# Where the score units of the next image stand: two of them moved ahead of the second group norm

## The chip, the cores and the metric

The kernel runs on one core of a Trainium2 chip. A core has five engines that run beside each other, each with its own instruction stream: TensorE for matmuls (PE in the profile, its weight loads PEld), VectorE (DVE), ScalarE (ACT), GpSimd (POOL) and SyncE (SP), which issues most of the DMAs. The engines wait for each other by semaphores. The metric is the device time of one execution in microseconds (us).

## The reference, cut to what matters

Input and output are four images of 256 channels by 64 x 64 pixels, f32. Two layers follow each other.

```python
# layer 0: attention over all 4096 pixels of an image
q = einsum('oc,bcn->bno', wq, xf) + bq            # 32 channels
k = einsum('oc,bcn->bon', wk, xf) + bk
attn = softmax(einsum('bnd,bdm->bnm', q, k), axis=-1)
v = einsum('oc,bcn->bon', wv, xf) + bv
x = gamma[0] * einsum('bcn,bmn->bcm', v, attn) + x
# layer 1
y = x + ls1 * cluster(group_norm(x, gn1_w, gn1_b), ...)
hdn = conv1x1(group_norm(y, gn2_w, gn2_b), mlp_w1, mlp_b1)      # 256 -> 1024
y = y + ls2 * conv1x1(gelu(hdn), mlp_w2, mlp_b2)                # 1024 -> 256
z = relu(batch_norm(y * dw_w, ...))
z = relu(batch_norm(conv1x1(z, pw_w), ...))                     # 256 -> 256
```

A group norm takes mean and variance over all channels and pixels of one image, so nothing behind it can start before the last pixel is there.

## The kernel before, in words

An image of 4096 pixels is cut into eight blocks of 512 (`NBLK`, `NB`). The four images go through three stages each: the attention's weighting, the cluster part, and the multilayer part (`mlp`, L1514), which holds the two 1 x 1 convolutions with the GELU between them, and the pointwise convolution. Every instruction of an engine stands in the order in which the Python code records it: nothing is moved by a scheduler. The order is written out by hand, and work of the next image is put between work of this one.

**Score units.** The attention's scores of an image are computed in 64 units: eight query blocks by eight key groups (`GRP`). A unit has two halves of 128 x 1024 scores, each two matmuls of 128 x 512 (`products`, L415) into one of two banks of the pool `ps_s` (each 128 x 2 x 512), and ACT copies each half into a buffer in SBUF (`kept`, L432). `score(u, hooks, later)` (L470) first calls `begun(u)` (L400), which issues the load of the *next* unit's key tile on SP (`k_unit`, L394, L398; two buffers for key tiles), then issues the matmuls of both halves, the first copy, and leaves the second copy in `hooks` and the running maximum over keys in `later`: four DVE instructions a unit (L492), two for unit 0. The first eight units of an image belong to its first query block; for images 1 to 3 they are computed during the previous image's stages, unit 0 at the end of its cluster part (L1393) and units 1 to 7 in its multilayer part.

**The end of the cluster part.** `cluster` adds its result to the image tiles in sixteen pieces. For half of them ACT scales the matmul's result (L1362) and POOL adds it (L1363), for the other half DVE does both (L1350). DVE then takes statistics of each piece (L1331). Between them, `fill(n)` runs parts of the next image's value projection (L375). Unit 0 of the next image comes last, and `cluster` returns.

**The second group norm (gn2).** `group_norm` (L270) combines the statistics on DVE (L274), averages over partitions by two tiny matmuls (L276, L277), and after one more average (L287), a square root on ACT (L199) and a reciprocal it gives scale and shift. `fill` puts value projections between. Then `norm(0)` scales block 0 (L1547) and forms differences of its quarters (L1614 to L1617).

**The multilayer part.** For each block `nb` there are four steps `j`, one for a quarter of the hidden channels, written (nb, j) below. `first` (L1683) does the first convolution of a step by `seven` (L1715), seven products of 128 x 256 in place of eight, in three banks of `ps_s`; DVE adds the parts (L1725) and ACT applies the GELU (L1689). `second_by_seven` (L1643) does the second convolution of the step before in seven products (L1651) and some sums on POOL (L1658 to L1663); `slots` says how many of those seven stand at which of four places inside the next `first`: (0, 2, 2, 3) or, behind a score, (3, 1, 2, 1). After step 0, `finish` adds the block before into the image tile (L1780), and after step 1 its ReLU runs on ACT (L1771) and the input of the block after is formed by DVE (`norm(nb + 1)`, L1547) and POOL. Step 2 is followed by the pointwise convolution of the block before, and the output leaves by DMA (L1607).

The dictionary `at` (L1825) says behind which step which score unit is computed:

```python
at = {(u, 3): u for u in range(1, 7)} | {(7, 2): 7}
if blocks < NBLK:                       # image 2: its last block is done later
    at |= {(6, 1): 6, (6, 2): 7}
    del at[6, 3]
```

The maxima that `score` leaves in `maxima` are taken out one at a time by `rest()` (L1818), four a block in blocks 0 to 6, around steps 2 and 3.

**Buffers.** The score buffers, the image tiles (two blocks each), the inputs of the blocks (`xn2`) and some others share one pool, `spool`, of 13 buffers of 8 KB a partition. A tile gets a buffer when it is first asked for, in the order of the code, and the first instruction that writes it waits until the last reader or writer of the buffer's former tile is done.

## Time and profile before

| what | value |
|---|---|
| median of 3 runs | 3199.19 us (3198.45 to 3201.14) |
| profiled execution: own time, span | 3196.98 us, 3195.0 us |
| PE busy | 3085.5 us, 97% of the span |
| DVE busy | 2537.0 us, 79% |
| POOL busy | 2260.6 us, 71% |
| ACT busy | 1734.8 us, 54% |
| granted TensorE clock, mean | 0.99 |

The profile is of one execution, and all its times count from the start of the span. A line of it names the engine, the line of the kernel, the tile written and those read; in brackets behind a line of the timeline stands how long the engine had been idle, and what ended that. The multilayer parts of images 0, 1 and 2 begin with the first product of block 0 at 623.6, 1408.9 and 2197 us. [...] a product of 128 x 256 (two passes) starts 0.43 us after the one before when nothing holds it up.

### The profile page before, as it was taken

What the parts mean: (1) busy time and instruction counts of PE and PEld (TensorE: products, weight loads), DVE (VectorE), ACT (ScalarE), POOL (GpSimd) and SP (SyncE); (2) the same over time, 40 slices, a digit from 0 to 9 for tenths busy, and PEclk for the clock granted to TensorE, in tenths of its full rate; (3) what the DMA queues carried; (4) which work ended last, traced back from release to release, by engine and by line L of the source; (5) the groups of instructions that cost most, each with busy time, mean ns of one, the idle gap of its engine ahead of it and who ended that gap; (6) DMA issues with size and microseconds to landing.
All of it is one profiled execution on the core that took longest, in us unless ns stands there. A gap on an engine that the chain in (4) does not pass through costs nothing.

```text
span 3195.0 us, 40473 instructions
## 1 busy us (share of the span) xinstructions
PE 3085.5 (97%) x13890; PEld 2445.7 (77%) x13890; DVE 2537.0 (79%) x3649; ACT 1734.8 (54%) x2719; POOL 2260.6 (71%) x2127
## 2 busy tenths in 40 slices
PE   7999999999999999999999999999999999998999
PEld 5777887788677787768867788786876787875786
DVE  3888888677788888867778888877778888887675
ACT  4556654545556665445555666544556566654444
POOL 3888886378488888547848888855766888883663
PEclk8999999999999999999999999999999999999999
DMA  5122126100112123510011222431111112150000
GB/s 164 40 63 63 60 61 182 63 21 30 47 50 63 53 60 94 155 50 28 23 56 44 66 60 63 111 123 50 30 44 43 54 60 64 56 149 2 14 21 27
DMA packets 105868, 200.33 MB, mean 63 GB/s; under 512 B 14416, under 2 KB 30400, under 8 KB 104128
## 3 DMA queue, kind: packets, MB, share of 16 engines
q1 hardware_dynamic: 101856, 181.94, 17.9%
q0 software_dynamic: 2976, 14.70, 2.5%
q8 instruction: 110, 1.80, 0.2%
q10 hardware_dynamic: 832, 1.11, 0.1%
q14 instruction: 94, 0.77, 0.1%
HBM read 149.37 MB, written 48.34 MB: 62 GB/s over the span
## 4 chain that ended last, share of the span: by engine, by line
PE 42%; POOL 24%; DVE 19%; issue 8%; ACT 6%; DMA 1%; POOLq 0%; SPq 0%; ACTq 0%; DVEq 0%
PE mo L1651 10%; POOL acc L595 9%; PE av L679 6%; PE hq L1734 5%; DVE top L444 5%; DVE s L583 4%; POOL t L595 4%; POOL s L595 4%; DVE t L616 3%; PE hp L1734 3%; PE hr L1734 3%; PE fv L1225 3%; PE sc L420 3%; POOL acc L611 2%; PE vp L375 2%
## 5 line engine op out<-in xcount | busy, mean ns | idle before, releaser
L433 ACT COPY s<-sc 128x1024 f32<-128x1024 f32 x512 | 514.8, 1011 | 506.3 <-PE sc L420 500.1
L583 DVE TENSOR_TENSOR s<-s,hold 128x1024 f32<-128x1024 f32 x512 | 598.7, 1209 | 28.9 <-ACT hold L566 15.0
L595 POOL TENSOR_TENSOR s<-t,s 128x512 f32<-128x512 f32 x224 | 303.5, 1355 | 356.1 <-DVE t L616 287.6
L679 PE MATMUL av<-t,v 128*128 128x256 f32 x1792 | 464.8, 382 | 12.8 <-DVE t L616 11.7
L679 PE MATMUL av<-s,v 128*128 128x256 f32 x1792 | 460.8, 379 | 2.2 <-ACT s L589 2.2
L595 POOL TENSOR_TENSOR acc<-acc,t 128x512 f32<-128x512 f32 x352 | 461.2, 1329 | 0.0
L679 PE MATMUL av<-s,sum 128*128 128x256 f32 x1792 | 459.5, 379 | 0.0
L420 PE MATMUL sc<-q,k 128*128 128x512 f32 x1024 | 405.6, 480 | 36.8 <-DMA k<-k 10.5
L444 DVE TENSOR_TENSOR top<-sc,top 128x1024 f32<-128x1024 f32 x326 | 397.8, 1220 | 29.7 <-ACT s L433 24.8
L1689 ACT ACTIVATE hs<-hs,pv_s 128x256 f32<-128x256 f32 x496 | 232.3, 502 | 343.5 <-DVE hs L1725 343.5
L616 DVE TENSOR_TENSOR t<-s,hold 128x1024 f32<-128x1024 f32 x224 | 272.7, 1217 | 159.3 <-ACT s L592 71.0
L679 PEld LDWEIGHTS av<-t,v 128*128 128x128 f32 x1792 | 338.4, 190 | 70.1 <-DVE t L616 21.4
L1651 PE MATMUL mo<-hs,w 128*128 128x256 f32 x1512 | 385.3, 381 | 0.0
L679 PEld LDWEIGHTS av<-s,v 128*128 128x128 f32 x1792 | 340.3, 190 | 57.8 <-ACT s L589 2.6
L679 PEld LDWEIGHTS av<-s,sum 128*128 128x128 f32 x1792 | 339.4, 189 | 54.5 <-issue 1.9
L1651 PEld LDWEIGHTS mo<-hs,w 128*128 128x128 f32 x1512 | 283.0, 190 | 47.2 <-ACT hs L1689 6.4
L595 POOL TENSOR_TENSOR t<-s 128x512 f32<-128x512 f32 x224 | 295.7, 1320 | 17.6
L420 PEld LDWEIGHTS sc<-q,k 128*128 128x128 f32 x1024 | 176.6, 190 | 144.0 <-DVE top L444 70.2
L592 ACT ACTIVATE s<-s 128x1024 f32<-128x1024 f32 x256 | 267.5, 1045 | 1.2
L1725 DVE TENSOR_TENSOR hs<-hq,hs 128x256 f32<-128x256 f32 x496 | 198.8, 421 | 79.2 <-PE hq L1734 69.3
L588 ACT ACTIVATE hold<-s 128x512 f32<-128x512 f32 x224 | 135.1, 603 | 221.5 <-DVE s L583 221.4
L679 PE MATMUL av<-t,sum 128*128 128x256 f32 x896 | 231.7, 381 | 0.0
(299 smaller groups left out, 5349.1 us busy)
## 6 DMA issues: line engine op xcount, KB each, us to landing
k<-k SPq DMA_DIRECT2D x256, 256.0 KB, 2.7
x<-in_x SPq DMA_DIRECT2D x62, 512.0 KB, 6.6
out<-xn SPq DMA_DIRECT2D x62, 256.0 KB, 2.1
att<-t SPq DMA_DIRECT2D x56, 256.0 KB, 3.9
x<-att POOLq DMA_DIRECT2D x12, 1024.0 KB, 8.7
q<-q SPq DMA_DIRECT2D x32, 256.0 KB, 4.1
w<-in_w SPq DMA_DIRECT2D x8, 1024.0 KB, 10.3
rden<-row_rd SPq DMA_DIRECT2D x28, 256.0 KB, 3.7
```

Of the source, the lines that this page charges most:

```text
L420: nc.tensor.matmul(sc[:, r, :], k_s[:, (2 * h + r) * P : (2 * h + r + 1) * P], qs[u // GRP], start=True, stop=True,)
L433: nc.scalar.copy(slots[u][:, PAIR[h]].rearrange("p h r n -> p r h n"), tiles(sc))
L444: nc.vector.tensor_tensor(top, src, top if saved[nb] is None else saved[nb], ALU.max)
L583: nc.vector.tensor_tensor(sh, sh, mb.to_broadcast([P, 2, 2, QW]), ALU.subtract)
L592: nc.scalar.activation(s[:, PAIR[1]], s[:, PAIR[1]], AF.Exp)
L595: nc.gpsimd.tensor_tensor(out, x, y, op)
L616: nc.vector.tensor_tensor(t31[u], s[:, B11 : B22 + 1 : 2], b12.to_broadcast([P, 2, 2, QW]), ALU.add)
L679: nc.tensor.matmul(av[bank][:, half_ * QW : (half_ + 1) * QW], a[:, r], t[:, r], start=(g == 0 and r == 0 and i in (1, 7, 2, 4)), stop=(g ...
L1651: return nc.tensor.matmul(bank[:, half * HB : (half + 1) * HB], a[:, j], t, start=start, stop=stop)
L1689: nc.scalar.activation(src, src, AF.Gelu_apprx_tanh, bias=pvc("b1", P, j + 4 * (i > 1)))
L1725: nc.vector.tensor_tensor(dst, ps, term, ALU.add)
L1734: nc.tensor.matmul(out, w, x, start=True, stop=True)
```

## The change

Units 1 and 2 of the next image are computed right behind unit 0, at the end of `cluster`, and thus ahead of gn2's matmuls on TensorE and ahead of gn2's work on ACT; their key loads, and that of unit 3, come earlier on SP. In the multilayer part, five steps and not seven have a score behind them (four and not six of the steps (u, 3), and (7, 2) as before; for image 2, three and not five, and (6, 1) and (6, 2) as before): units 3 and 4 move up to the steps (2, 3) and (3, 3), and the steps (1, 3) and (4, 3) have none. The `slots` of the steps behind these two change with that. The maxima of units 1 and 2 wait in `maxima` with those of unit 0, so `rest()` finds work from block 0 on, and none in block 5.

```diff
+EARLY = 3
...
         nxt.q_block(0)
         nxt.k_unit(0)
         fill(1)
-        copies = []
-        nxt.score(0, copies, maxima)
-        copies.pop()()
+
+        for u in range(EARLY):
+            copies = []
+            nxt.score(u, copies, maxima)
+            copies.pop()()
         return stats2
...
-        at = {(u, 3): u for u in range(1, 7)} | {(7, 2): 7}
+        at = {(2, 3): 3, (3, 3): 4, (5, 3): 5, (6, 3): 6, (7, 2): 7}
         if blocks < NBLK:
             at |= {(6, 1): 6, (6, 2): 7}
             del at[6, 3]
```

Line numbers of the changed kernel are three higher up to L1392 and five higher behind it.

## The prediction

> **What bounds the kernel now.** I read the page's first two parts, then who waited for whom with TensorE as the waiter, then the timeline around the second group norm (gn2) of image 0, and then busy time by stretch.

> ```profile
> PE 3085.5 (97%) x13890; PEld 2445.7 (77%) x13890; DVE 2537.0 (79%) x3649; ACT 1734.8 (54%) x2719; POOL 2260.6 (71%) x2127
> ...
> PE gnm_gn L276 <- DVE mv_gn L274: 12.8, 3, 4.3
> ```

> TensorE is busy 97% of the span, so a change pays only if it takes matmul time out of a saturated stretch or fills one of the few holes. The second line is such a hole: three times, once for each image that has a successor, TensorE stands 4.26 us before the first matmul of gn2.

> ```profile
> 609.55 7.21 DVE L1331 BATCH_NORM_STATS2 st<-x 128x6 f32<-128x512 f32 x12
> ...
> 610.30 0.81 PE L420 MATMUL sc<-q,k 128*128 128x512 f32 x2
> ...
> 612.29 1.94 ACT L433 COPY s<-sc 128x1024 f32<-128x1024 f32 x2
> ...
> 612.44 0.73 PE L420 MATMUL sc<-q,k 128*128 128x512 f32 x2 [1.33 <-ACT cl L1362]
> ...
> 616.79 0.59 DVE L274 BATCH_NORM_AGGREGATE mv_gn<-st 128x2 f32<-128x96 f32 x1
> ...
> 617.43 0.59 PE L276 MATMUL gnm_gn<-mv_gn,left 128*128 128x1 f32 x2 [4.26 <-DVE mv_gn L274]
> ```

> The hole lasts from 613.17 to 617.43, and DVE's statistics end it. Unit 0's four score matmuls stand ahead of it; ACT copies each half out in 0.97.

> ```profile
> 613.20:617.40 4.20, 0.00 (x0) 0.00 (x0) 4.14 (x7) 1.03 (x2) 4.12 (x4) 0.88 0.00 0
> 617.40:623.60 6.20, 6.17 (x18) 5.24 (x19) 2.90 (x11) 2.18 (x4) 2.96 (x3) 0.53 0.00 0
> 623.60:636.20 12.60, 12.60 (x74) 8.61 (x73) 7.96 (x20) 5.78 (x12) 3.32 (x5) 1.00 0.46 166
> ```

> Columns: length, busy time (count) of PE, PEld, DVE, ACT, POOL, then the granted clock. After the idle stretch the clock is 0.53: the hole costs more than its length. The same pair stands at 1403 (0.56) and 2191 (0.52).

> [...] the clock halves at 616.39, after a 3.41 us window with under 0.05 us of matmul, and returns at 623.21. [...] the 256 KB key loads (L398) land 2.4 at least, 2.7 median, 4.5 at most after issue. [...]

> **The change, part by part (for one image; three have it).**

> *Removed from the multilayer part:* the scores behind steps (1,3) and (4,3). From the starts of the first product of each step: a scored step 3 takes 7.05 and the next step 0 4.77, together 11.8. Image 3 has no scores and takes the slot pattern that these two steps now get: 4.75 + 6.04 = 10.79. So 1.0 each, **-2.0**. After block 0, the step 0 of an unscored pattern took 6.51, 0.47 over, because a POOL factor (L1615) came late. At (4,3) POOL's factor ends at 761.77 and would be needed at about 762.3; bounds 0 to 0.47, I take **+0.1**.

> *Added ahead of gn2:* eight matmuls, four ACT copies, two key loads. Copies of unit 0 end at 613.26 and 614.23, so unit 1's halves run at 613.3 and 614.3 (two matmuls of 0.215 each), their copies end at 615.2 and 616.2. Unit 2 needs key tile 2, whose buffer unit 0 frees at 613.17; nothing stands before it on SP until 629.6, so it lands near 615.9. Its four matmuls issue by 616.8, 0.6 ahead of 617.43; the last copy ends near 618.7, ahead of ACT's next work (620.40). gn2's statistics are DVE's and POOL's and don't move. Cost **0**, hidden by the hole; each us by which the key lands later than 2.7 + 0.6 delays gn2 by one us (4.5: +1.2); below nothing it can't be.

> *Moved on DVE:* eight maxima of 0.69 to blocks 0 and 1. Step 2 with maxima takes 10.71, without 10.54. Block 1 now pays that 0.17, block 5 no longer does; block 0's step 3 has DVE gaps of 1.27. Sum **0** (bounds -0.2 to +0.3).

> *A buffer wait that the diff doesn't show:* two more of the 13 big buffers are taken before gn2, and the built program gives the input of block 5 the buffer of the image tile with blocks 2 and 3, last read by the relu of block 3 on ACT. In the trace DVE writes block 5's first half at

> ```profile
> 747.08 1.41 DVE L1547 TENSOR_SCALAR xn<-x,ga_gn,gb_gn 128x512 f32<-128x512 f32 x2
> 748.40 1.21 DVE L492 TENSOR_TENSOR top<-top,s 128x512 f32<-128x512 f32 x1
> ...
> 747.79 0.80 ACT L1771 ACTIVATE xn<-x,dw_e,dw_d 128x512 f32<-128x512 f32 x1
> ```

> and the relu ends at 748.59: DVE now stands 1.56. Behind it queue the second half, a maximum and step 2's additions; the first of these (749.53 to 749.95) frees the bank of TensorE's matmul at 750.63. With the maximum at its usual 0.75 the addition ends near 751.1, TensorE loses 0.47; with 1.2 it loses 0.75. The pointwise part has a stall of 0.12 to absorb. **+0.5**, bounds 0 and 1.56. The new waits of unit 4 and of blocks 3 and 4 on an output's DMA have a step or more in hand, as block 5's own unit has now: 0.

> *The clock:* with the hole filled the clock may stay full. An estimate from the trace: counting 0.215 a pass, the window at 2111 (about 0.36 busy) dropped the clock and the one at 2183 (0.38) didn't. A half unit is 0.43, so a 3.41 us window passes with three halves (0.378) and fails with two. Halves would lie at 610.3, 612.4, 613.3, 614.3, 615.9 and 616.4; sliding the window over them, somewhat under half of the positions catch only two. If the clock holds: gn2's first matmuls reach DVE in 0.7 (as gn1's do) rather than 1.06, the four passes of value projection before gnv (L287) take 0.9 rather than 1.9, so the statistics are ready 1.4 earlier, and the second product of block 0, at 624.05 now, waits only for DVE's L1615, ending at 623.77 - 1.37: **-1.5** (bounds -1.6 and 0).

> Sum for one image: -2.0 + 0.1 + 0 + 0 + 0.5 = **-1.4** with the clock dropped, **-2.9** with it held. Three images: -4.2 to -8.7; held in two of three, **-7.2**. On the profiled execution, whose span is 3195.0 and own time 3196.98, this gives 3187.8 and 3189.8; the median shown is 3199.19, 2.2 above that execution, so 3192.0.

> **Rivals.**

> *Clock drops anyway.* For: gaps of 1.7 (before unit 0's second half) and 1.2 (before key tile 2) remain, and the margin is one half unit. Against: the 0.38 window. -4.2 to -5.7 with one held: 3195.0 to 3193.5, within 0.2%.

> *The buffer wait eats it.* For: DVE has no gap from 741 to 749 in that block. If all 1.56 reaches TensorE: -2.0 + 0.1 + 1.56 = -0.3, about -1 in three: 3198 (3194 with the clock held). Against: TensorE has 0.7 of slack before the bank it needs.

> *The key load becomes the gate (slower).* [...] gn2 stands behind unit 2's matmuls, and those behind key tile 2. Landing L after 613.17, gn2 is late by L - 3.3, and the clock drops too. The 1.4 is gone at L = 4.7; slower by 0.2% (6.4 us) takes L = 6.9: 3206. Against: the longest of 256 key loads was 4.5, and no DMA runs between 600 and 629.

> **How the numbers follow.** About 0.2% (6.4 us) is what a measurement of this kernel tells from no change. Clock held in two or three images: 0.5 (3190.5 to 3192.0). Clock dropped in most: 0.3. Buffer wait in full: 0.1. Key load: 0.04. The rest, 0.06, is mostly a gain that I haven't seen. So faster 0.55, same 0.40, slower 0.05. Range: low with all clocks held and buffer and POOL waits nothing, -3.5 x 3 = -10.5, 3188.7, rounded to 3189.0; high 3198.5, just past the buffer rival.

> **What would show it.** The row "gnm_gn <- mv_gn" falls from 12.8 to under 2; eight L420 matmuls lie between 613 and 617; the clock in the 6 us after gn2's first matmul is 1.00 where it held; the steps behind (1,3) and (4,3) add to 10.8; a new wait of DVE L1547 on ACT L1771 of about 1.5, three times. I am wrong if gn2's first matmul starts later against the last statistics than now, if block 4's step 2 loses over 1 us, or if gn2 keeps the clock low in all three while the total still falls by 7.

## The result, and the profile after

The changed kernel takes 3192.68 us (median of 12 runs, 3188.03 to 3198.69), the kernel before beside it 3199.59 (12 runs, 3197.33 to 3203.37). The ratio is 0.9977, with a 95% interval of 0.997 to 0.9985: faster by 0.23%. The profiled execution of it has a span of 3188.8 us and an own time of 3191.02; that of before had 3195.0 and 3196.98.

The first part of the page has the same instructions on every engine as before; TensorE is busy 5.3 us less, in a span that is 6.2 shorter:

```profile
PE 3080.2 (97%) x13890; PEld 2442.4 (77%) x13890; DVE 2539.7 (80%) x3649; ACT 1734.9 (54%) x2719; POOL 2257.7 (71%) x2127
```

TensorE's waits (total, times, longest) show that the hole ahead of gn2 is gone. The row had 12.8 us in three waits:

```profile
PE gnm_gn L279 <- DVE mv_gn L277: 0.6, 2, 0.4
```

The timeline of the changed kernel at the same place in image 0 (start, length, engine, line, ..., in brackets the idle time before it):

```profile
612.73 0.82 PE L423 MATMUL sc<-q,k 128*128 128x512 f32 x2
...
614.71 3.77 ACT L436 COPY s<-sc 128x1024 f32<-128x1024 f32 x4
614.87 0.73 PE L423 MATMUL sc<-q,k 128*128 128x512 f32 x2 [1.32 <-ACT cl L1365]
615.63 2.15 SPq L401 DMA_DIRECT2D k<-k  x2
615.78 0.73 PE L423 MATMUL sc<-q,k 128*128 128x512 f32 x2 [0.18 <-ACT s L436]
616.70 0.73 PE L423 MATMUL sc<-q,k 128*128 128x512 f32 x2 [0.19 <-ACT s L436]
...
618.42 1.17 PE L423 MATMUL sc<-q,k 128*128 128x512 f32 x4 [0.99 <-DMA k<-k]
...
619.86 0.38 PE L279 MATMUL gnm_gn<-mv_gn,left 128*128 128x1 f32 x2 [0.27 <-DVE mv_gn L277]
```

The two units lie in the hole as forecast: unit 1's halves follow ScalarE's copies, unit 2 waits for its key tile, which is there 2.8 us after its load was issued, and gn2 starts 7.13 us after unit 0, exactly as before. What follows is the busy time by stretch, for image 0 and for image 2. The columns are PE, PEld, DVE, ACT, POOL, then the granted clock:

```profile
612.70:619.80 7.10, 4.21 (x14) 1.94 (x12) 7.07 (x12) 6.20 (x9) 6.90 (x6) 1.00 0.29 74
619.80:625.50 5.70, 4.47 (x21) 3.46 (x22) 3.70 (x14) 3.93 (x7) 3.04 (x3) 1.00 0.00 0
...
2177.50:2185.00 7.50, 5.36 (x14) 2.88 (x13) 7.09 (x12) 6.25 (x9) 7.28 (x6) 0.76 0.25 72
2185.00:2191.40 6.40, 6.40 (x19) 5.32 (x18) 3.23 (x12) 3.53 (x6) 2.69 (x3) 0.50 0.00 0
```

In images 0 and 1 the clock stayed at 1.00, in image 2 it fell to 0.50, as it had fallen in all three before. There the matmuls of unit 2 itself ran at the low clock (its four took 2.05 against 1.17 in image 0), and gn2 came 0.35 later. In the traces of before and after every stretch of one granted clock that ends inside the span lasts a whole multiple of 3.413 us (1 to 579 of them); such a piece of 3.41 us is called a window here.

To say where the time went, I put the starts of the same matmuls of both executions side by side and took the differences of successive ones. All three images agree to 0.02 outside gn2's own stage:

| stretch | before | after | difference, image 0 / 1 / 2 |
|---|---|---|---|
| unit 0 to the first product of (0, 1): hole and gn2 | 20.00 | 18.82 | -1.18 / -1.08 / +0.54 |
| step (1, 0) | 6.51 | 6.85 | +0.34 / +0.33 / +0.32 |
| step (1, 2) | 10.54 | 10.72 | +0.18 each |
| steps (1, 3) and (2, 0) | 11.78 | 10.79 | -0.99 / -1.01 / -1.01 |
| step (4, 2) | 10.71 | 11.03 | +0.32 / +0.31 / +0.31 |
| steps (4, 3) and (5, 0) | 11.82 | 10.95 | -0.87 / -0.85 / -0.86 |
| step (5, 2) | 10.72 | 10.53 | -0.19 each |
| unit 0 to the next image's first weighting product | 250.74 | 248.28 | -2.46 / -2.36 / -0.78 |

The columns before and after are image 0's. The last row adds to -5.6 in three images; the other 0.6 of the span is a balance of differences elsewhere, where the programs are the same (+2.4 ahead of image 0's unit 0, -1.2 and -2.4 in the weighting and cluster parts of images 1 and 2, +0.5 in the last image). Part of it lies where the clock fell in one execution and not in the other; I didn't follow the rest.

Two losses were in it. The first I had seen coming; it is the wait of VectorE at the input of block 5, in the timeline of image 0:

```profile
748.52 0.80 ACT L1776 ACTIVATE xn<-x,dw_e,dw_d 128x512 f32<-128x512 f32 x1
...
749.35 1.41 DVE L1552 TENSOR_SCALAR xn<-x,ga_gn,gb_gn 128x512 f32<-128x512 f32 x2 [1.46 <-ACT xn L1776]
...
751.75 1.13 PE L1739 MATMUL hr<-xn,w 128*128 128x256 f32 x4 [0.23 <-DVE hs L1730]
```

The relu ends at 749.32, VectorE has then stood 1.46, and of that TensorE loses about 0.3. The second I had missed. It is at the head of block 1:

```profile
649.00 0.73 POOL L1619 TENSOR_TENSOR xn<-xn 128x256 f32<-128x256 f32 x1
649.37 0.92 DVE L495 TENSOR_TENSOR top<-top,s 128x512 f32<-128x512 f32 x1
...
649.82 1.05 POOL L1620 TENSOR_TENSOR xn<-xn 128x256 f32<-128x256 f32 x1
...
650.92 0.70 PE L1739 MATMUL hp<-xn,w_abcd 128*128 128x256 f32 x2 [0.54 <-POOL xn L1620]
```

A maximum that now stands behind first(0, 3) runs on VectorE at the moment when GpSimd forms the second factor of block 1. That factor takes 1.05 where it took 0.72 before, and the second product of the block waits for it 0.54 instead of 0.20, as in this line of before:

```profile
649.33 0.70 PE L1734 MATMUL hp<-xn,w_abcd 128*128 128x256 f32 x2 [0.20 <-POOL xn L1615]
```

### The profile page after: what moved, and what is told of

The parts are those of the page before. It is cut to its first block, busy times and chain, and to the rows that moved or that the text cites. A ratio compares the mean times of both kernels' runs of the same rounds, so it can differ in the third digit from the quotient of the medians.

```text
span 3188.8 us, 40484 instructions
## 1 busy us (share of the span) xinstructions
PE 3080.2 (97%) x13890; PEld 2442.4 (77%) x13890; DVE 2539.7 (80%) x3649; ACT 1734.9 (54%) x2719; POOL 2257.7 (71%) x2127
## 3 DMA queue, kind: packets, MB, share of 16 engines
q10 hardware_dynamic: 832, 1.11, 0.1%
## 4 chain that ended last, share of the span: by engine, by line
PE 40%; POOL 23%; DVE 20%; issue 8%; ACT 7%; DMA 2%; SPq 0%; POOLq 0%; ACTq 0%; DVEq 0%
PE mo L1656 9%; POOL acc L598 9%; PE av L682 5%; DVE top L447 5%; DVE s L586 5%; PE hq L1739 5%; POOL t L598 4%; POOL s L598 4%; DVE t L619 4%; PE hr L1739 3%; PE hp L1739 3%; PE fv L1228 3%; PE sc L423 2%; POOL acc L614 2%; ACT s L595 2%
## 5 line engine op out<-in xcount | busy, mean ns | idle before, releaser
L682 PE MATMUL av<-t,v 128*128 128x256 f32 x1792 | 463.7, 381 | 12.8 <-DVE t L619 12.1
```

What stands on the lines that cost most here:

```text
L682: nc.tensor.matmul(av[bank][:, half_ * QW : (half_ + 1) * QW], a[:, r], t[:, r], start=(g == 0 and r == 0 and i in (1, 7, 2, 4)), stop=(g ...
```

## The experiments

All times below are device times beside the kernel before on the same chip; the profiles are of one execution each. Where I give "sum in three images", it is the last row of the table above for that kernel, against the profile of before.

**The clock alone.** The kernel before, no unit moved, with sixteen matmuls that nobody reads put into the hole:

```diff
+        def warm(n):
+            spare = ps_a.tile([P, NB], F32, tag="a1", name=f"spare_{b}_{n}")
+            for _ in range(n):
+                nc.tensor.matmul(spare, qs[0][:, :P], qs[0], start=True, stop=True)
...
         nxt.score(0, copies, maxima)
         copies.pop()()
+        nxt.warm(16)
```

> The kernel before, with no unit moved; only sixteen score matmuls of unit 0 repeated into a bank that nobody reads, behind unit 0, so that TensorE works from 613.2 to 616.6 instead of standing. My theory: what the hole costs beyond its length is the halved clock. gn2's first matmul stays 7.13 us behind unit 0's first, and from there to the second product of (0, 0) to the first of (0, 1) it takes 1.1 less in each image with a successor (the changed kernel showed -1.17 and -1.08 where its clock held), so about -3.4 us in all, every other step equal within 0.05. Rival, that the clock matters less than the chain of DVE and ACT behind the mean: -0.5 or less in each image, under -1.5 in all. Rival, that the removed score steps are the whole gain: 0.

Measured: 3194.48 us, ratio 0.9982 (0.9975 to 0.999). From unit 0 to the first product of (0, 1) it takes 18.86 in each of the three images, where before had 20.00, 19.93 and 20.14; the sum in three images is -3.4, and every other step is equal within 0.05. Its timeline of TensorE, and one stretch of its busy time:

```profile
615.08 3.80 PE L473 MATMUL spare<-q 128*128 128x512 f32 x16
619.49 0.38 PE L276 MATMUL gnm_gn<-mv_gn,left 128*128 128x1 f32 x2 [0.61 <-DVE mv_gn L274]
```

```profile
619.50:625.20 5.70, 4.49 (x22) 3.46 (x23) 3.76 (x13) 2.65 (x5) 3.01 (x3) 1.00 0.00 0
```

So matmuls that compute nothing, in a time when TensorE would have stood, are worth 1.1 to 1.3 us an image. Both rivals fall. The timed gain of 5.4 is larger than 3.4, but its interval (3.2 to 8.0) holds 3.4.

**One unit less in the hole.**

```diff
-EARLY = 3
+EARLY = 2
...
-        at = {(2, 3): 3, (3, 3): 4, (5, 3): 5, (6, 3): 6, (7, 2): 7}
+        at = {(1, 3): 2, (2, 3): 3, (3, 3): 4, (5, 3): 5, (6, 3): 6, (7, 2): 7}
```

> The changed kernel with one unit less moved: units 0 and 1 ahead of gn2, unit 2 again behind step (1, 3). My theory: in each of three images one removal of 1.0 stays (steps (4, 3) and (5, 0)), the steps (1, 3) and (2, 0) go back to 11.8; the hole from 614.7 to gn2's first matmul holds one 3.41 us window of under 0.3 busy at nearly every position, so the clock drops in all three images: gn2 to (0, 1) as in the kernel before, within 0.1. The wait for the relu at (4, 2), +0.3, needs the changed order of buffers and may or may not stay. Together -0.4 to -0.9 an image, -1 to -3 in all against the kernel before, 3 to 5 slower than the changed kernel. Rival, that any work in the hole holds the clock: gn2's stage 1.1 shorter too, -5 in all.

Measured: 3196.2 us, ratio 0.999 (0.9981 to 0.9998); sum in three images -1.0. The steps are as expected: (1, 3) and (2, 0) back at 11.8, (4, 3) and (5, 0) at 10.95, and both losses, (1, 0) at 6.86 and (4, 2) at 11.03, stay. The clock fell in all three images, but its cost was not that of before: to the first product of (0, 1) it took 19.12, 20.71 and 19.94, so -0.9, +0.8 and -0.2 against before. VectorE's waits for gn2's two averages (L283, L201) show where it ran low: 0.70 and 1.26 in image 0, so it fell between the two, 1.11 and 1.66 in image 1, 1.10 and 1.66 in image 2, against 0.70 and 0.61 in image 0 of the changed kernel, where it held. "As before within 0.1" was wrong. That any work in the hole holds the clock is excluded.

**The maxima of block 0 put off.**

```diff
         def rest():
-            if maxima:
+            if maxima and (nb, j) != (0, 3):
                 maxima.pop(0)()
```

> The changed kernel, with no running maximum taken in step 3 of block 0; they wait for blocks 1 and 2. My theory: the 0.33 that (1, 0) lost comes from the maximum behind first(0, 3): beside it GpSimd's second factor of block 1 takes 1.05 and not 0.72, and TensorE's second product waits for that. So (1, 0) goes back from 6.84 to 6.51 in each of the three images; block 2 step 2 keeps its maxima. -1.0 us in all against the changed kernel. Rival, that the (1, 0) loss comes from the changed slot pattern or from the buffers: (1, 0) stays at 6.84, 0 in all.

In the timeline of this kernel the same factor and product of image 0 are

```profile
651.04 0.73 POOL L1620 TENSOR_TENSOR xn<-xn 128x256 f32<-128x256 f32 x1
...
651.83 0.70 PE L1739 MATMUL hp<-xn,w_abcd 128*128 128x256 f32 x2 [0.21 <-POOL xn L1620]
```

Step (1, 0) takes 6.52 in each of the three images, all other steps stay, and the two maxima cost nothing where they went: -0.97 in all. The time, 3192.99 us (ratio 0.9979, 0.9972 to 0.9986), doesn't show it against the changed kernel's 3192.68: 1 us is below what these medians resolve. The step is what decides here.

**The buffer wait taken away.** Not by taking the wait, but by changing which buffer block 5's input gets: unit 4 is asked for after it, as in the kernel before.

```diff
-        at = {(2, 3): 3, (3, 3): 4, (5, 3): 5, (6, 3): 6, (7, 2): 7}
+        at = {(2, 3): 3, (4, 3): 4, (5, 3): 5, (6, 3): 6, (7, 2): 7}
```

> The changed kernel with unit 4 again behind step (4, 3) and the step (3, 3) without a score in its place, so five blocks have a score as before. Unit 4's buffer is then taken after the one for the input of block 5, which gets that of block 2's input and not that of the image tile with blocks 2 and 3. My theory: the wait of VectorE at the input of block 5 for ScalarE's relu is gone; step (4, 2) takes 10.54 (no maxima in it now) instead of 11.03, block 5's step 2 takes 0.2 more for its maxima; steps (4, 3) and (5, 0) add to 11.8 again and (3, 3) and (4, 0) to 10.8 to 10.95 instead of 11.8. -0.3 an image, -0.9 us in all against the changed kernel. Rival, that the +0.31 of step (4, 2) comes from the maxima or something else in that block: step (4, 2) stays at 10.7 or above by itself and nothing is won in all.

VectorE's waits (total, times, longest), first of the changed kernel, then of this one:

```profile
DVE xn L1552 <- ACT xn L1776: 7.3, 5, 1.5
```

```profile
DVE xn L1552 <- ACT xn L1776: 2.9, 2, 1.5
```

Three waits of about 1.46 are gone: 4.4 of the 7.3 us. Step (4, 2) takes 10.54, steps (3, 3) and (4, 0) add to 10.79, (4, 3) and (5, 0) to 11.8, step (5, 2) takes 10.72. Against the changed kernel that is -0.49 - 1.02 + 0.84 + 0.19 = -0.48 an image, where 0.3 was expected; the rest is GpSimd's late factor, which costs the step behind (4, 3) 0.15 and the step behind (3, 3) nothing. Of the 0.49, 0.17 is the maxima, so the wait itself was worth 0.32. The time is 3190.99 us, ratio 0.9972 (0.9963 to 0.9981). Its profiled execution lost the clock in all three images (VectorE waits 1.66 for gn2's second average in each), and the hole and gn2 then took 19.95, 20.77 and 20.78: 0 to 0.8 more than before.

**The clock held for certain.** The changed kernel with the two gaps of 1.3 and 1.0 us in the hole filled:

```diff
-            scs = [products(u, h) for h in range(2)]
+            scs = [products(u, 0)]
+            if b and u == 0:
+                warm(4)
+            scs.append(products(u, 1))
...
         for u in range(EARLY):
             copies = []
+            if u == 2:
+                nxt.warm(4)
             nxt.score(u, copies, maxima)
```

> The changed kernel with eight score matmuls of unit 0 repeated into a bank that nobody reads: four between the halves of unit 0, four ahead of unit 2, where TensorE stands 1.3 and 1.2 us. My theory: every 3.41 us window of the hole then has over 0.4 of matmul, so the clock holds in all three images: from unit 0's first matmul to the first of (0, 1) 18.7 to 18.9 in each, where the changed kernel had 18.8 in images 0 and 1 and 20.7 in image 2. Against the profile of the changed kernel -1.8 us in these stages, in the timed median -1 to -3 (its executions lose the clock in one or two of three images). gn2's first matmul no later than 7.13 after unit 0's first. Rival, that the repeated matmuls delay the bank changes or the key load: gn2 later by 0.3 or more in each image. Rival, that the drop in image 2 has another cause than the thin window: it drops again.

Measured: 3189.47 us, ratio 0.9968 (0.9955 to 0.998). Hole and gn2 take 18.85, 18.88 and 18.88, gn2 stands 7.13 behind unit 0 in each image, and the sum in three images is -7.4. Busy time by stretch in image 2, where the changed kernel had 0.76 and 0.50:

```profile
2180.00:2187.10 7.10, 6.12 (x22) 3.35 (x20) 7.05 (x12) 6.22 (x9) 6.93 (x6) 1.00 0.26 76
2187.10:2192.80 5.70, 4.43 (x21) 3.43 (x22) 3.71 (x13) 3.89 (x7) 3.07 (x3) 1.00 0.00 0
```

So the thin window (0.31 of matmul in the changed kernel's image 2, by the count below) was the cause there, and holding the clock is worth 1.8.

**A fourth unit.** Unit 3 ahead of gn2 as well, step (2, 3) without a score. The load of unit 4's key tile is left behind step (2, 3), since that part of the keys isn't computed yet ahead of gn2.

```diff
-EARLY = 3
+EARLY = 4
...
-            if u + 1 < units:
+            if u + 1 < units and (not b or u != 3):
                 k_unit(u + 1)
...
-        at = {(2, 3): 3, (3, 3): 4, (5, 3): 5, (6, 3): 6, (7, 2): 7}
+        at = {(3, 3): 4, (5, 3): 5, (6, 3): 6, (7, 2): 7}
...
+                if nxt and (nb, j) == (2, 3):
+                    nxt.k_unit(4)
```

> The changed kernel with unit 3 ahead of gn2 as well, step (2, 3) without a score; the load of unit 4's key tile stays behind step (2, 3). My theory: the hole is full. Unit 3's halves wait for ScalarE's copies of unit 2 (0.97 each), so its last matmul ends near 621.5 on the changed kernel's scale and gn2's first matmul comes 1.5 to 1.9 later against the statistics; 1.0 is won at (2, 3) and (3, 0). +0.5 to +0.9 an image, about +2 in all against the changed kernel, less 1 to 1.7 if the clock now holds in all three images. Rival, that more units ahead of gn2 are still hidden: gn2 at 7.13, -1.0 an image, -3 in all.

Measured: 3216.46 us, ratio 1.0055 (1.0042 to 1.0068), 17 slower than the kernel before. The part that was forecast came: gn2 stands 8.96, 9.11 and 8.96 behind unit 0 instead of 7.13, with the clock held in all three (VectorE waits 0.61 for gn2's second average in each), and steps (2, 3) and (3, 0) save 0.9. But step (1, 3) takes 10.71, 12.11 and 12.01 instead of 4.75, which neither theory had. Its timeline in image 0:

```profile
678.52 0.72 POOL L598 TENSOR_TENSOR sum<-v,sum 128x256 f32<-128x256 f32 x1 [6.36 <-DMA out<-xn]
...
679.98 0.70 PE L1656 MATMUL mo<-hs,w 128*128 128x256 f32 x2 [4.01 <-POOL hs L1663]
```

With one more score buffer taken early, the third tile of GpSimd's sums gets, in the built program, the buffer of block 0's input, which is free only once block 0's output has left by DMA. GpSimd stands 6.36 for it, its sums for the second convolution queue behind, and TensorE stands 4.01 for those; behind that its products start 0.65 to 0.85 apart and no longer 0.43, so the clock fell too. It is the same mechanism as the wait at block 5, with a DMA in place of the relu. The wait for the relu itself now comes at block 3's input too: the row of VectorE's waits for it goes from five (7.3 us) to eight (11.7 us), and step (2, 2) takes 0.3 more. The sum in three images is +16.1.

**The key tile late.** The changed kernel with unit 2's key load issued twice:

```diff
-            nc.sync.dma_start(out=ks[u].bitcast(F32), in_=stacked("k", g))
+            for _ in range(2 if b and u == 2 else 1):
+                nc.sync.dma_start(out=ks[u].bitcast(F32), in_=stacked("k", g))
```

> The changed kernel with the load of unit 2's key tile issued twice, one behind the other, so that the tile is there one load later. My theory of the gate: the margin between unit 2's last matmul and gn2 is 0.3 (619.3 to 619.8), so gn2's first matmul is late by the delay less 0.3: with 2.7 for the second load +2.2 to +2.5 an image, and TensorE stands over 3 us, so the clock drops in every image and its gain of 1.1 is gone too: +3.3 to +4 an image where it had held; 3 to 6 slower than the kernel before in all (3201 to 3206). If the two loads overlap on the queues, the delay is under 1 and the loss under 1 an image. Rival, that the hole has more room than 0.3: under +1 an image with a delay of 2.7.

```profile
613.57 3.42 SPq L402 DMA_DIRECT2D k<-k  x3
...
618.94 2.05 PE L424 MATMUL sc<-q,k 128*128 128x512 f32 x4 [3.56 <-DMA k<-k]
...
620.78 0.42 PE L279 MATMUL gnm_gn<-mv_gn,left 128*128 128x1 f32 x2
```

Measured: 3204.06 us, ratio 1.0015 (1.0008 to 1.0021): slower than the kernel before. In this timeline of image 0, unit 2 starts 5.4 after the first issue instead of 2.8. TensorE has then stood 3.56, and its four matmuls take 2.05 instead of 1.17, so the clock is down. gn2 stands 10.12, 9.98 and 10.43 behind unit 0: 3 later, for a load that was 2.6 later. The sum in three images is +4.9. The gate that the third rival named is real and lies close: 2.6 for the load and 0.9 for the slower matmuls, less the 3.0 that arrived, leave half a microsecond as all the room there is.

**All three repairs together.** No maxima in step 3 of block 0, unit 4 behind (4, 3), the eight filling matmuls; the diff is that of the three kernels above.

> The changed kernel with the three additions together: no maxima in step 3 of block 0, unit 4 behind (4, 3) and no score behind (3, 3), and the eight repeated matmuls that hold the clock. If the three are independent: (1, 0) 6.51, (4, 2) 10.54, gn2's stage with the clock held in all three images; -1.0 -1.4 and -1 to -3 against the changed kernel, so -3.5 to -5.5, 3187.2 to 3189.2, ratio to the kernel before 0.996 to 0.997. Rival, that the order of buffers or the maxima of blocks 1 and 2 bring a new wait: a step that is longer than in each of the single changes.

Measured: 3187.84 us (3185.64 to 3188.93), ratio 0.9962 (0.995 to 0.9975). The steps add as if each were alone: (1, 0) 6.52, (4, 2) 10.53, hole and gn2 18.86, 18.86 and 18.90 (gn2 0.2 late in image 2, for a reason I didn't follow), no step longer than in the single kernels; the sum in three images is -9.6. Its median is the lowest here; its interval overlaps that of the kernel that only holds the clock (0.9955 to 0.998).

## Why the prediction was right, and where it was not

The time forecast, 3192.0, was 0.7 from the one measured, and the main mechanisms were those named. The sum behind it was too good by a fifth, though: -5.6 in three images by the trace, against -7.2. The maxima cost 1.0 that wasn't in the sum, and the clock gave 1.3 less than in it; the buffer wait made up for 0.6. The timed difference, -6.9 with an interval of 4.8 to 9.6, holds both sums, so that the median came within 0.7 is partly luck.

*Removal, -2.0 and +0.1: right.* The two pairs of steps gave -0.99 and -0.87, together -1.86 against -1.9. The image without scores was the right model for the pattern that the unscored steps take, and the factor of GpSimd cost 0.15.

*The added units in the hole, 0: right where the clock held.* Halves at 614.9, 615.8, 616.7 and 618.4 in steps of ScalarE's copies, the key tile 2.8 after its issue, gn2 7.13 behind unit 0. The slack of 0.6 was about 0.5.

*The maxima, 0 with bounds of -0.2 and +0.3: this step failed.* It measured +0.33 in (1, 0), +0.18 in (1, 2), -0.19 in (5, 2): +0.3, at the upper bound, 1 us in three images. The two smaller terms are the 0.17 that I had. What went wrong is "block 0's step 3 has DVE gaps of 1.27": I looked for room on VectorE alone. The maximum found its gap, but GpSimd works beside that gap on the factor that the next product waits for, and side by side both took longer: the maximum took 0.92 (0.68 at the input of block 5) and ended 0.55 after the factor that had begun ahead of it; the next factor took 1.05 (0.73 without the maximum) and ended 0.58 after the maximum. What made them longer was not shown.

*The buffer wait, +0.5 with bounds of 0 and 1.56: the mechanism right, the size 0.31.* VectorE stood 1.46 where I had 1.56. The matmul behind the addition started at 751.75, which is 0.38 later against the start of block 4 than before (750.63, and 0.74 for the shift of the block), where I had 0.47 to 0.75: the maximum in the queue, at 750.68, took 0.68 and not 0.75 to 1.2. The rest of the step won 0.07 back. The experiment with the other order of buffers gave 0.32. The second rival, that all of it reaches TensorE, is excluded; the fourth unit shows what the same kind of wait costs when it lands on GpSimd.

*The clock, -1.5 if held: mechanism right, size -1.2 and -1.1.* Filling the hole with matmuls that compute nothing gives the same amount, so it is the clock and not the units. The missing 0.3 is in the chain that follows. In the changed kernel's timeline of image 0, and further down image 2, where the clock had fallen:

```profile
621.57 1.26 POOL L1537 TENSOR_TENSOR w<-w,w 128x512 f32<-128x512 f32 x1
...
622.39 0.47 DVE L296 TENSOR_SCALAR ga_gn<-pc_s,rstd_gn 128x2 f32<-128x2 f32 x1
...
2188.76 0.23 DVE L296 TENSOR_SCALAR ga_gn<-pc_s,rstd_gn 128x2 f32<-128x2 f32 x1
```

The chain behind the mean is 1.35 earlier, as I had it from gn1's, and runs into the last of GpSimd's four weight sums, which it missed before: the small scale on VectorE takes 0.47 here and ends with GpSimd's instruction (622.86 against 622.84). Among the images with a successor it took 0.47 to 0.53 in all twelve of the ten profiles where the clock held and gn2 was at its place (0.37 in a thirteenth, where gn2 was 0.2 late), and 0.23 in all fourteen where the clock had fallen. With the fourth unit, gn2 comes 1.8 later, the sums are done, and it takes 0.23 at full clock; the stretch from gn2 to the first product is then 3.60 instead of 3.94. So the 0.24 is that meeting. About 0.1 of the shortfall is left without a cause.

*The clock, 0 if dropped: wrong.* I had taken the hole of before as the worst case. Here the clock fell while units stood in the hole, and unit 2's matmuls ran at half clock ahead of gn2 (2.05 against 1.17): +0.5 in image 2; in the three images of the kernel with the other order of buffers, where it fell too, it was 0 to +0.8. So a dropped image gains 0.8 in all, not 1.4, and held and dropped differ by 1.7 rather than 1.5. A gn2 that starts later was one of the signs that I had named for being wrong, and in image 2 it did start later, by 0.35.

*Held in two of three: so it was in the profile.* By my count of 0.215 a pass, the thinnest windows in images 0 and 1 had exactly three halves, 0.38, and the clock held; that in image 2 had 0.31 and it fell. (The window of before at 2183 that I had put at 0.38, as the case against the first rival, has 0.43 when the matmuls that run into its start are counted, so it was weaker support than it looked.) How often the timed executions held it isn't known directly. With the clock held for certain the median is 3.2 lower than the changed kernel's, which would be two dropped images of three, but the two medians come from different comparisons and are uncertain by about 2 each. The mean clock of the timed executions points to one or two: its median is 0.990 to 0.991 before, where the profile lost it in all three images, 0.994 with the hole of before filled, 0.9915 for the changed kernel and 0.993 with its two gaps filled, though losses elsewhere in the program weigh on these means too. So the first rival may well have been as common as the forecast case in the timed runs.

*The rival that would have made it slower* needs a key tile 2 to 3 us later. One repeated load did that, at +4.4 us against the kernel before. I had let the clock enter that sum as a gain lost; it also slowed unit 2 (2.05 and not 1.17), so gn2 was late by more than the load.

## What to carry to other kernels

An idle stretch of TensorE can cost more than its length: here the clock over the 6.2 us behind a hole of 4.26 was 0.53. Filling it so that the clock stayed at 1.00 was worth 1.1 to 1.3 us an image by itself, beside the 1.9 that the moved work saved. A fill that is just at the border is a matter of luck: with 0.38 of matmul in its thinnest window the clock held here in two images, with 0.31 it fell in the third. Before moving small work into a gap of one engine, look at what the engine beside it does in that time (a maximum on VectorE beside a factor on GpSimd took 0.92 and not 0.68, and the next factor 1.05 and not 0.73), and at which instruction waits for that one. When tiles of a common pool are asked for in another order, list who gets whose buffer and when its last reader ends: here the same change of order cost 0.3 us in one place, and one tile more cost 6 to 7 us in another.

## What the runs showed of the hardware that was not expected

A two-column scale on VectorE took 0.47 to 0.72 us instead of 0.23 when GpSimd was in the middle of a sum of 1.26. In the changed kernel's images 0, 1 and 3 and in image 0 of the kernel with the sixteen filling matmuls it ended 0.02 to 0.03 us behind GpSimd's instruction (622.86 against 622.84, 1404.78 against 1404.76, 2952.84 against 2952.82, 622.54 against 622.51). The reciprocal on VectorE just ahead of it, beside the same sum, took its usual 0.16, so it isn't every instruction of VectorE that gets longer. That a scale of 128 x 2 can take twice its usual time is what I hadn't counted with; what held it was not shown.
